# A recommender forward pass on one core: splitting the small tables by identity matmuls instead of VectorE subtractions

## The chip, the core and the metric

The kernel runs on one core of a Trainium2 chip. The metric is the device time of one execution in microseconds (us); lower is better. The kernel before took 5261.35 us, the median of four runs (5259.9 to 5262.66).

The engines named here: TensorE (PE in the profile; PEld is its weight loading), VectorE (DVE), ScalarE (ACT), GpSimd (POOL), which issues the indirect gathers, and SyncE (SP), which issues the plain DMAs. Each works through its own instructions in the order of the program and waits for the others by semaphores. SBUF is the on-chip memory, PSUM the memory that matmuls write.

## The reference

16384 samples. Each takes the mean of 32 rows of a word table (50000 x 300), the means of 20 rows each of three multi-hot tables (1000, 5000 and 10000 rows of 64), and one row each of four one-hot tables (100, 50, 20 and 1000 rows of 64). The 748 features go through a three-layer network. A "wide" scalar per row of the small tables is summed beside it.

```python
tok = word_emb[token_idx].mean(axis=1)
e1 = emb_mh1[mh1_idx].mean(axis=1)        # e2, e3 alike
o1 = emb_oh1[oh1_idx]                     # o2, o3, o4 alike
emb = jnp.concatenate([tok, e1, e2, e3, o1, o2, o3, o4], axis=1)
wide = (wide_mh1[mh1_idx].sum(axis=(1, 2)) + ... + wide_oh4[oh4_idx][:, 0])[:, None]
h = jax.nn.relu(emb @ W1 + b1)            # 748 -> 1024
h = jax.nn.relu(h @ W2 + b2)              # -> 512
h = jax.nn.relu(h @ W3 + b3)              # -> 256
return jax.nn.sigmoid(h @ Wd + bd + wide)
```

## The kernel before

**Tiles and ticks.** The batch is cut into 128 tiles of 128 samples (loop over `t`, line 476). Each tile has 11 steps (`STEPS`, loop over `i`, line 489). This text calls one step a tick and numbers ticks through the tiles: tick 0 is the first step of tile 0, tick 11 the first of tile 1. The order of all instructions is written out by hand (`tc.manual_schedule()`). In one tick the program issues, in this order: the one-hot masks of the next tick (`one_hots`, line 294, VectorE, two instructions), the count matmuls of this tick (`counts`, line 312, twelve matmuls, eight in a tile's last tick) with their eviction by ScalarE (line 319), some steps of the table conversion (only in tiles 0 and 1), the token gathers and sums, a share of the small-table sums of the tile before (`small_sums`, line 337), and, from tile 5 on, a share of the network of the block of four tiles before (`mlp`).

**Tokens.** The 32 word rows of a sample are gathered in 16 groups of two: GpSimd issues two indirect DMAs (line 224), and VectorE adds the two rows to a running sum (lines 211, 213, 215). The adds of a group are issued three groups later (`TOK_LAG`), and there are six buffers `tok_rows`: the first gather of group n+6 needs the buffer of group n, so it waits for the adds of group n. The running sum `own` lies in PSUM, as does the `iota` that the masks are compared with.

**Small tables.** The seven small tables are 138 slices of 128 rows of 65 values (64 and the wide one). A tile's small lookups are turned into counts for every slice row (one-hot masks multiplied on TensorE), and the counts are multiplied with the slices, which lie in SBUF as `terms`: three bf16 terms that together hold twice the f32 value. `small_sums` reads a slice of `terms` for every matmul, from tick 11 on. It takes slices 0 to 15 in tick 11 and reaches slice 134 in tick 19.

**Making the terms.** `convert_tables` fills `terms` while ticks 3 to 17 run, paced by `TABLE_PACE`: `tables_on_chip.to(TABLE_PACE * (t * STEPS + i - 2))` (line 501) advances the generator until it has made that many steps. The tables come in six parts of 23 slices, loaded by SyncE (lines 152 and 158) into two buffers (`raw`, tags "even" and "odd"); VectorE clears the incomplete slices first (line 157). Each part takes three steps: ScalarE casts to bf16 (line 180), then VectorE subtracts the term just made from the f32 rows (line 177) and ScalarE casts the remainder, twice. The next part's load is issued when a part begins, into the buffer of the part before.

**Buffers around it.** The one-hot masks have two buffers, so the masks of tick T+1 wait for the count matmuls of tick T-1. The counts' PSUM tile `pc` has one, so the count matmuls of tick T wait for the eviction of tick T-1. The PSUM tag "ph" has two buffers; the key transposes, the feature transposes and the layers use it, and in ticks 3 to 19 it is free.

Of the kernel before, what the change touches and what calls it, by code (L numbers as in the profile page):

```python
# [8 lines left out]
F32 = mybir.dt.float32  # L9
BF16 = mybir.dt.bfloat16  # L10
# [3 lines left out]
AF = mybir.ActivationFunctionType  # L14
ALU = mybir.AluOpType
AX = mybir.AxisListType

P = 128
N_TOK, TOK_D = 32, 300
N_MH, EMB = 20, 64  # L20
ROW = EMB + 1
# [4 lines left out]
HALF = P // 2  # L26
N_SMALL = 3 * N_MH + 4
ONEHOT = 6
STEPS = -(-HALF // ONEHOT)
CHUNK_WORK = 1  # L30
TABLE_PACE = 1.2
LAYER_TIME = 10


# [12 lines left out]
def kernel(  # L47
# [21 lines left out]
    nc = tc.nc  # L69
# [6 lines left out]
    slices, n_h = {}, 0  # L76
# [6 lines left out]
    const = ctx.enter_context(tc.tile_pool(name="const", bufs=1))  # L83
# [8 lines left out]
    ps_h = ctx.enter_context(tc.tile_pool(name="ps_h", bufs=2, space=bass.MemoryType.PSUM))  # L92
# [17 lines left out]
    ident = const.tile([P, P], F32, name="ident")  # L110
# [3 lines left out]
    scale = const.tile([P, NK], F32, name="scale")  # L114
# [20 lines left out]
    at = 0  # L135
# [4 lines left out]


    terms = const.tile([P, n_h, 3 * ROW], BF16, name="terms")
    PART = n_h // 6

    def load_tables(part0, tag):
        raw = xp.tile([P, PART, ROW], F32, name="raw", tag=tag)
        for f in SMALL:
            table, (h0, h1) = tables[f], slices[f]
            full, rest = divmod(table.shape[0], P)
            a, b = max(h0, part0), min(h0 + full, part0 + PART)  # L150
            if a < b:
                nc.sync.dma_start(
                    out=raw[:, a - part0 : b - part0, :],
                    in_=table[(a - h0) * P : (b - h0) * P, :].rearrange("(h p) d -> p h d", p=P),
                )
            if rest and part0 <= h0 + full < part0 + PART:
                nc.vector.memset(raw[:, h0 + full - part0, :], 0.0)
                nc.sync.dma_start(out=raw[0:rest, h0 + full - part0, :], in_=table[full * P :, :])
        return raw

    def convert_tables():


        tags = ("even", "odd")
        raws = [load_tables(k * PART, tags[k]) for k in range(2)]
        yield
        for part in range(n_h // PART):
            rows = raws[part]
            if 1 <= part < n_h // PART - 1:
                raws.append(load_tables((part + 1) * PART, tags[(part + 1) % 2]))  # L170
            for c in range(3):
                term = [
                    terms[:, part * PART : (part + 1) * PART, k * ROW : (k + 1) * ROW]
                    for k in range(3)
                ]
                if c:
                    nc.vector.scalar_tensor_tensor(
                        rows, rows, 2.0 if c == 1 else 1.0, term[c - 1], op0=ALU.mult, op1=ALU.subtract
                    )
                nc.scalar.activation(term[c], rows, AF.Copy, scale=2.0 if c == 0 else 1.0)  # L180
                yield 1

    w1_sb = const.tile([P, NK, D1], F32, name="w1_sb")
    w2_sb = const.tile([P, M1, D2], F32, name="w2_sb")
# [7 lines left out]
    def load_weights():  # L192
        for k, rows in enumerate(chunk_rows):
            at = 0
            for a, b in rows:
                nc.sync.dma_start(out=w1_sb[at : at + b - a, k, :], in_=w1[a:b, :])
                at += b - a
        nc.sync.dma_start(out=w2_sb, in_=w2.rearrange("(k p) m -> p k m", p=P))
        nc.sync.dma_start(out=w3_sb, in_=w3.rearrange("(k p) m -> p k m", p=P))
        for sb, dram in ((wd_sb, wd), (b1_sb, b1), (b2_sb, b2), (b3_sb, b3), (bd_sb, bd)):  # L200
            nc.sync.dma_start(out=sb, in_=dram)
# [33 lines left out]
    def last_tokens():  # L235
        for group in under_way:
            add_up(*group)
# [19 lines left out]
    def lookup_keys(ix):  # L257

        pairs = NSUB // 2
        low = keyp.tile([P, pairs, 2, N_SMALL], I32, name="low", tag="low")  # L260
        nc.vector.tensor_single_scalar(low, ix, P - 1, op=ALU.bitwise_and)
        nc.vector.tensor_single_scalar(ix, ix, 7, op=ALU.logical_shift_right)
        keys = keyp.tile([P, pairs, 2, 2 * N_SMALL], BF16, name="keys", tag="keys")
        for r in range(pairs):
            view = keys[:, r].rearrange("p w (f c) -> p w f c", f=2)
            nc.vector.tensor_copy(view[:, 0], low[:, r])
            nc.vector.tensor_add(view[:, 1], ix[:, r], first)
        return keys
# [17 lines left out]
    def one_hots(sc, s, i):  # L286

        b = i * ONEHOT
        rows = min(ONEHOT, HALF - b)
        row1 = ohp.tile([P, ONEHOT, P], BF16, name="row1")  # L290
        slice1 = ohp.tile([P, ONEHOT, n_h], BF16, name="slice1")
        for w, (one, n) in enumerate(((row1, P), (slice1, n_h))):
            shape = [P, rows, n // 2, 2]
            nc.vector.tensor_tensor(  # L294
                one[:, 0:rows, :].rearrange("p i (n d) -> p i n d", d=2),
                iota[:, 0:n].rearrange("p (n d) -> p n d", d=2).unsqueeze(1).to_broadcast(shape),
                sc[:, s // 2, w, s % 2, b : b + rows, :].unsqueeze(2).to_broadcast(shape),
                ALU.is_equal,
            )
        return row1, slice1  # L300

    def counts(cnt, hot, i):

        b = i * ONEHOT
        rows = min(ONEHOT, HALF - b)
        n = rows // 2
        pc = ps_c.tile([P, 2, 2, 512], F32, name="pc")
        for k in range(rows):
            for f in range(2):
                half = slice(f * HALF, (f + 1) * HALF)  # L310
                at = k % n * n_h
                nc.tensor.matmul(  # L312
                    pc[:, f, k // n, at : at + n_h],
                    hot[0][half, k, :],
                    hot[1][half, k, :],
                    start=True,
                    stop=True,
                )
        nc.scalar.activation(  # L319
            cnt[:, :, b : b + rows, :].rearrange("l f (g k) h -> l f g (k h)", g=2),  # L320
            pc[:, :, :, 0 : n * n_h],
            AF.Copy,
            scale=0.5,
            saturate=False,
        )
# [116 lines left out]
    def sums_by_step(gen):  # L442
# [5 lines left out]
        n_second = slices["e3"][1] - slices["e2"][0]  # L448
        for i in range(STEPS):

            steps = STEPS - (n_pairs - 1)
            upto = n_first + -(-n_second * i // steps)
# [15 lines left out]
    sizes = [NSUB] * (tiles // NSUB - 1) + [NSUB - 2, 1, 1]  # L468
    it, ix = load_indices(0)
    tables_on_chip = convert_tables()  # L470
    next(tables_on_chip)
    tables_on_chip = Paced(tables_on_chip)
# [3 lines left out]
    for t in range(tiles + 1):  # L476
# [10 lines left out]
        else:  # L487
            last_tokens()
        for i in range(STEPS):
            if t < tiles:  # L490
# [3 lines left out]
                if s == 2 and i == 0 and t + NSUB < tiles + 1:  # L494
                    next_keys = lookup_keys(ix)
                if i < STEPS - 1:
                    hot = one_hots(sc, s, i + 1)
                elif t + 1 < tiles:
                    hot = one_hots(next_sc if s == NSUB - 1 else sc, (s + 1) % NSUB, 0)
                counts(cnt, hot_now, i)  # L500
                tables_on_chip.to(TABLE_PACE * (t * STEPS + i - 2))
                if t == 1 and i == STEPS - 1:
                    load_weights()
# [61 lines left out]
```

## Time and profile before

| | |
|---|---|
| median of four runs | 5261.35 us |
| the profiled execution | 5264.25 us |
| its span, first to last instruction | 5262.4 us |
| PE busy | 5088.7 us, 97% |
| POOL busy | 3887.9 us, 74% |
| DVE busy | 3767.2 us, 72% |
| ACT busy | 2445.6 us, 46% |
| DMA engines | mean 124 GB/s, 0.47 of their time in the middle of the span |
| table casts, ACT L180 | 18 instructions, 128x1495, median 1468 ns, 19.6 to 80.6 us |
| table subtractions, DVE L177 | 12 instructions, 128x1495, median 1707 ns, 21.1 to 78.9 us |
| granted TensorE clock, mean | 0.99 |

How to read it: busy time is the union of an engine's instructions, and the issuing of a gather counts as busy time on POOL although a fixed gap of 0.30 us follows each one. An engine busy for 97% is not necessarily the one that sets the end, since matmul ends are modelled and an engine may keep pace with another. A line such as "idle before, releaser" says which event ended the engine's idle time. The page's seven rows of costliest groups belong to work that goes on in every tile; the table conversion lies in the first 82 us alone.

### The profile page before, as it was taken

The page shows a single profiled execution, that of the slowest core. Times are in us where ns is not written, and L with a number is a line of the kernel's source. Part 1 is how long each engine was busy: PE and PEld are TensorE (multiplying, and loading weights), DVE is VectorE, ACT ScalarE, POOL GpSimd, SP SyncE. Part 2 cuts the span into 40 slices and gives each one's busy share as a digit, 9 for nine tenths or more (in the row PEclk, how much of TensorE's full clock was granted, in tenths as well). Part 3 has the DMA queues.
Part 4 walks back from the last instruction along what each step waited for, and adds up shares of the span by engine and source line. Part 5 has one row for each costly group of instructions (what it writes and reads, how often), then busy time and mean ns, then how long its engine had stood idle before and what let it go on. Part 6 is the DMA issues. An engine that isn't in the chain of part 4 may idle for free.

```text
span 5262.4 us, 104252 instructions
## 1 busy us (share of the span) xinstructions
PE 5088.7 (97%) x41320; PEld 3162.3 (60%) x41320; DVE 3767.2 (72%) x8014; ACT 2445.6 (46%) x1938; POOL 3887.9 (74%) x4103
## 2 busy tenths in 40 slices
PE   4799999999999999999999999999999999999999
PEld 3565565665656656665655666556566556666558
DVE  8777777777777777777777777777777777777752
ACT  5444444444444444444444444444444444444432
POOL 7777777777777777777777777777777777777761
PEclk8899999999999999999999999999999999999999
DMA  6444444444444444444444444444444444444431
GB/s 190 125 125 124 126 126 126 126 125 124 126 126 126 126 124 126 126 126 126 126 124 125 126 126 126 125 124 126 126 126 126 124 126 126 126 126 126 124 99 34
DMA packets 252890, 652.60 MB, mean 124 GB/s; under 512 B 119009, under 2 KB 119524, under 8 KB 252399
## 3 DMA queue, kind: packets, MB, share of 16 engines
q0 software_dynamic: 196608, 629.41, 44.5%
q1 hardware_dynamic: 55791, 16.53, 1.4%
q8 instruction: 323, 5.29, 0.4%
q14 instruction: 168, 1.38, 0.1%
HBM read 645.59 MB, written 0.07 MB: 123 GB/s over the span
## 4 chain that ended last, share of the span: by engine, by line
PE 43%; DMA 21%; DVE 14%; issue 13%; POOL 9%; ACT 0%; DVEq 0%; SPq 0%; POOLq 0%; ACTq 0%
PE ph L388 23%; DMA tok_rows<-in_word_emb_dram,it 21%; PE pg L337 14%; POOL tok_rows L224 9%; PE pc L312 5%; DVE own L215 4%; DVE own L213 2%; DVE slice L294 2%; DVE x L379 1%; DVE row L294 1%; DVE g L343 1%; PE po L413 1%; DVE own L211 0%; DVE g L215 0%; PE po L417 0%
## 5 line engine op out<-in xcount | busy, mean ns | idle before, releaser
L224 POOL DMA_INDIRECT tok_rows<-in_word_emb_dram,it x4096 | 3887.0, 949 | 1294.3 <-issue 735.6
L319 ACT ACTIVATE cnt<-pc 128x1656 fp8e3<-128x1656 f32 (+1 forms) x1408 | 2120.7, 1506 | 2046.7 <-PE pc L312 2037.0
L337 PE MATMUL pg<-terms,cnt 128*128 128x195 bf16 x17664 | 1850.0, 254 | 89.0 <-DVE g L343 86.6
L337 PEld LDWEIGHTS <-cnt 128*128 128x128 fp8e3 x17664 | 1598.6, 144 | 235.8 <-issue 81.9
L388 PE MATMUL ph<-x,w_sb 128*128 128x512 f32 (+5 forms) x3264 | 1467.7, 579 | 3.6 <-DVE x L379 2.8
L215 DVE TENSOR_TENSOR own<-own,tok_rows 128x300 f32<-128x300 f32 x1792 | 857.8, 479 | 679.7 <-DMA tok_rows<-in_word_emb_dram,it 646.0
L388 PE MATMUL ph<-h,w_sb 128*128 128x512 f32 (+2 forms) x2720 | 1211.0, 573 | 0.0
L213 DVE TENSOR_TENSOR own<-own,tok_rows 128x300 f32<-128x300 f32 x1920 | 918.9, 479 | 363.9 <-DMA tok_rows<-in_word_emb_dram,it 311.4
L312 PEld LDWEIGHTS <-row 64*128 64x128 bf16 x16384 | 502.0, 95 | 1038.4 <-DVE slice L294 249.5
L294 DVE TENSOR_TENSOR row<-own,sc 128x768 bf16<-128x768 bf16 (+1 forms) x1408 | 762.3, 541 | 187.9 <-PE pc L312 118.6
L312 PE MATMUL pc<-slice,row 64*128 64x138 bf16 x16384 | 758.8, 224 | 69.0 <-DVE slice L294 35.3
L388 PEld LDWEIGHTS ph<-x,w_sb 128*128 128x128 f32 (+1 forms) x3264 | 563.8, 194 | 410.4 <-issue 398.1
L294 DVE TENSOR_TENSOR slice<-own,sc 128x828 bf16<-128x828 bf16 (+1 forms) x1408 | 797.3, 566 | 0.0
L388 PEld LDWEIGHTS ph<-h,w_sb 128*128 128x128 f32 x2720 | 463.1, 192 | 318.8 <-issue 316.9
L397 ACT ACTIVATE h<-ph,b_sb 128x512 f32<-128x512 f32 (+2 forms) x476 | 315.6, 663 | 687.3 <-PE ph L388 682.3
L343 DVE TENSOR_REDUCE g<-pg 128x130 f32<-128x390 f32 (+1 forms) x512 | 259.0, 506 | 145.2 <-PE pg L337 144.1
L379 DVE TENSOR_SCALAR x<-pt,scale 128x512 f32<-128x512 f32 (+4 forms) x204 | 137.0, 712 | 3.4 <-PE pt L378 2.7
L378 PE MATMUL pt<-ident,g 128*128 128x128 f32 (+1 forms) x768 | 104.4, 275 | 3.0 <-DVE x L379 2.3
L211 DVE TENSOR_TENSOR own<-tok_rows 128x300 f32<-128x300 f32 x128 | 61.7, 482 | 47.6 <-DMA tok_rows<-in_word_emb_dram,it 45.0
L378 PEld LDWEIGHTS pt<-ident,g 128*128 128x128 f32 (+1 forms) x768 | 85.3, 140 | 8.1 <-DVE x L379 6.9
L215 DVE TENSOR_TENSOR g<-own,tok_rows 128x300 f32<-128x300 f32 x128 | 60.2, 470 | 22.8 <-DMA tok_rows<-in_word_emb_dram,it 18.1
L413 PE MATMUL po<-h,wd_sb 128*1 128x512 f32 (+2 forms) x136 | 60.9, 566 | 0.3
(34 smaller groups left out, 290.0 us busy)
## 6 DMA issues: line engine op xcount, KB each, us to landing
tok_rows<-in_word_emb_dram,it POOLq DMA_INDIRECT x4096
ix<-in_idx_dram SPq DMA_DIRECT2D x128, 32.0 KB
w_sb<-in_W_dram SPq DMA_DIRECT2D x6, 512.0 KB
raw<-in_mh_dram SPq DMA_DIRECT2D x3, 747.5 KB
it<-in_idx_dram SPq DMA_DIRECT2D x32, 64.0 KB
w_sb<-in_W_dram SPq DMA_DIRECT2D x1, 2048.0 KB
raw<-in_mh_dram SPq DMA_DIRECT2D x1, 617.5 KB
out_dram<-h SPq DMA_DIRECT2D x31, 2.0 KB
```

The costliest lines, as they stand in the source:

```text
L213: nc.vector.tensor_add(tok_sum, tok_sum, a)
L215: nc.vector.tensor_add(to, tok_sum, b)
L224: nc.gpsimd.indirect_dma_start(out=rows[:, r * TOK_D : (r + 1) * TOK_D], out_offset=None, in_=word, in_offset=bass.IndirectOffsetOnAxis(ap ...
L294: nc.vector.tensor_tensor(one[:, 0:rows, :].rearrange("p i (n d) -> p i n d", d=2), iota[:, 0:n].rearrange("p (n d) -> p n d", d=2).unsque ...
L312: nc.tensor.matmul(pc[:, f, k // n, at : at + n_h], hot[0][half, k, :], hot[1][half, k, :], start=True, stop=True,)
L319: nc.scalar.activation(cnt[:, :, b : b + rows, :].rearrange("l f (g k) h -> l f g (k h)", g=2), pc[:, :, :, 0 : n * n_h], AF.Copy, scale=0 ...
L337: nc.tensor.matmul(pg[:, j, :], by_slice[:, :, h], terms[:, h, :], start=(h == h0), stop=(h == h1 - 1))
L343: nc.vector.tensor_reduce(g[:, at : at + n * ROW].rearrange("p (f d) -> p f d", f=n), pg[:, 0:n, :].rearrange("p f (c d) -> p f d c", c=3) ...
L378: nc.tensor.transpose(pt[:kk, s * P : (s + 1) * P], chunk(g, k), ident)
L379: nc.vector.tensor_scalar(x[:kk, k, 0:n], pt[:kk, 0:n], scale[:kk, k : k + 1], None, ALU.mult)
L388: nc.tensor.matmul(ph[:, 0:n], weights[:kk, k, m * P : (m + 1) * P], src[:kk, k, 0:n], start=(k == 0), stop=(k == len(kks) - 1),)
L397: nc.scalar.activation(dst[:, m, 0:n], ph[:, 0:n], AF.Relu, bias=bias[:, m : m + 1])
```

## The change

The rows of the small tables are no longer changed in place by VectorE. The remainder of a slice is made by TensorE in PSUM: the f32 rows times an f32 identity, plus the finished terms times a bf16 matrix of -0.5 on the diagonal (`minus_half`, made once by VectorE). As the terms hold twice the value, that sum is the value less the terms, and ScalarE casts it from PSUM with a scale of 2. The work goes in pieces of seven slices (455 columns, 20 pieces) in place of parts of 23, three terms of three different pieces in one step: the third term of piece s-2, the second of s-1, the first of s. There are 22 steps. Parts that are loaded together have 21 slices (seven parts, the last of 12), and a part's buffer is loaded anew, for the part after next, when its last piece has its third term. `TABLE_PACE` goes from 1.2 to 1.3, so that the steps lie in ticks 3 to 19: two each in ticks 3, 6, 9, 13 and 16, one in the others.

```diff
 ONEHOT = 6
+SPLIT = 7
+PART = 3 * SPLIT
...
-TABLE_PACE = 1.2
+TABLE_PACE = 1.3
...
     terms = const.tile([P, n_h, 3 * ROW], BF16, name="terms")
-    PART = n_h // 6
+    minus_half = const.tile([P, P], BF16, name="minus_half")
+    nc.vector.tensor_single_scalar(minus_half, ident, -0.5, op=ALU.mult)
...
-        raws = [load_tables(k * PART, tags[k]) for k in range(2)]
+        parts = range(0, n_h, PART)
+        raws = [load_tables(parts[k], tags[k]) for k in range(2)]
         yield
-        for part in range(n_h // PART):
-            rows = raws[part]
-            if 1 <= part < n_h // PART - 1:
-                raws.append(load_tables((part + 1) * PART, tags[(part + 1) % 2]))
-            for c in range(3):
-                term = [
-                    terms[:, part * PART : (part + 1) * PART, k * ROW : (k + 1) * ROW]
-                    for k in range(3)
-                ]
-                if c:
-                    nc.vector.scalar_tensor_tensor(
-                        rows, rows, 2.0 if c == 1 else 1.0, term[c - 1], op0=ALU.mult, op1=ALU.subtract
-                    )
-                nc.scalar.activation(term[c], rows, AF.Copy, scale=2.0 if c == 0 else 1.0)
-                yield 1
+        pieces = []
+        for k, part0 in enumerate(parts):
+            for at in range(part0, min(part0 + PART, n_h), SPLIT):
+                pieces.append((k, at, min(at + SPLIT, part0 + PART, n_h)))
...
+        def make(p, c):
+            if c == 0:
+                nc.scalar.activation(term(p, 0), rows(p), AF.Copy, scale=2.0)
+                return
+            _, a, b = pieces[p]
+            left = ps_h.tile([P, SPLIT, ROW], F32, name="left", tag="ph")[:, 0 : b - a, :]
+            nc.tensor.matmul(left, ident, rows(p), start=True, stop=False)
+            for k in range(c):
+                nc.tensor.matmul(left, minus_half, term(p, k), start=False, stop=(k == c - 1))
+            nc.scalar.activation(term(p, c), left, AF.Copy, scale=2.0)
+
+        for step in range(len(pieces) + 2):
+            for c in (2, 1, 0):
+                if 0 <= step - c < len(pieces):
+                    make(step - c, c)
+            k, _, b = pieces[min(max(step - 2, 0), len(pieces) - 1)]
+            if step >= 2 and b in parts and k + 2 < len(parts):
+                raws.append(load_tables(parts[k + 2], tags[k % 2]))
+            yield 1
```

More of the change, by code (lines that the diff above doesn't have):

```diff
@@ L164, in convert_tables, with term, rows @@
         tags = ("even", "odd")
-        raws = [load_tables(k * PART, tags[k]) for k in range(2)]
+        parts = range(0, n_h, PART)
+        raws = [load_tables(parts[k], tags[k]) for k in range(2)]
         yield
-        for part in range(n_h // PART):
-            rows = raws[part]
-            if 1 <= part < n_h // PART - 1:
-                raws.append(load_tables((part + 1) * PART, tags[(part + 1) % 2]))
-            for c in range(3):
-                term = [
-                    terms[:, part * PART : (part + 1) * PART, k * ROW : (k + 1) * ROW]
-                    for k in range(3)
-                ]
-                if c:
-                    nc.vector.scalar_tensor_tensor(
-                        rows, rows, 2.0 if c == 1 else 1.0, term[c - 1], op0=ALU.mult, op1=ALU.subtract
-                    )
-                nc.scalar.activation(term[c], rows, AF.Copy, scale=2.0 if c == 0 else 1.0)
-                yield 1
+        pieces = []
+        for k, part0 in enumerate(parts):
+            for at in range(part0, min(part0 + PART, n_h), SPLIT):
+                pieces.append((k, at, min(at + SPLIT, part0 + PART, n_h)))
+        def term(p, c):
+            _, a, b = pieces[p]
+            return terms[:, a:b, c * ROW : (c + 1) * ROW]
+        def rows(p):
+            k, a, b = pieces[p]
+            return raws[k][:, a - parts[k] : b - parts[k], :]
+        def make(p, c):
+            if c == 0:
+                nc.scalar.activation(term(p, 0), rows(p), AF.Copy, scale=2.0)
+                return
+            _, a, b = pieces[p]
+            left = ps_h.tile([P, SPLIT, ROW], F32, name="left", tag="ph")[:, 0 : b - a, :]
[11 more added lines that the diff above has]
+            yield 1
     w1_sb = const.tile([P, NK, D1], F32, name="w1_sb")
```

## The prediction

> **What bounds the kernel now.** PE's 97% invites the answer "TensorE". I asked who waits. First the page's group of the gathers, then POOL's waits between 300 and 5000 us:
>
> ```profile
> L224 POOL DMA_INDIRECT tok_rows<-in_word_emb_dram,it x4096 | 3887.0, 949 | 1294.3 <-issue 735.6
> ...
> POOL tok_rows L224 <- issue: 667.7, 2192, 0.3
> POOL tok_rows L224 <- DVE own L215: 292.5, 960, 0.3
> ```
>
> The last number is the longest wait: never above 0.3 us, which is the fixed gap after every gather. So in 4700 us nothing holds POOL up. The gathers' own view from 100 to 5000 us shows the pace:
>
> ```profile
> L224 POOL DMA_INDIRECT tok_rows<-in_word_emb_dram,it x3918: 942/946/1193, 99.2 to 4999.4; - x196
> ```
>
> (4999.4 - 99.2) / 3917 = 1.251 us a gather, 40.0 us a tile of 32. TensorE keeps up with that; it becomes the bound only after about 5018 us, when POOL's gaps grow beyond 0.3, and works off the rest. Hence what POOL loses early moves the end one for one. It does lose early. At 1.251 us the 65th gather would start at 3.20 + 64 x 1.251 = 83.3 us; the timeline has it at 94.22. Of these 10.9 us, 0.15 is the first gather's own length. The rest is seen in the timeline of the first tile (start, duration):
>
> ```profile
> 21.09 1.72 DVE L177 SCALAR_TENSOR_TENSOR raw<-raw,terms 128x1495 f32<-128x1495 f32 x1 [4.21 <-ACT terms L180]
> 22.10 1.52 POOL L224 DMA_INDIRECT tok_rows<-in_word_emb_dram,it  x1 [0.30 <-issue]
> ...
> 24.78 1.71 DVE L177 SCALAR_TENSOR_TENSOR raw<-raw,terms 128x1495 f32<-128x1495 f32 x1
> 25.22 2.08 POOL L224 DMA_INDIRECT tok_rows<-in_word_emb_dram,it  x1 [0.30 <-issue]
> ```
>
> A gather under way when L177 runs ends 0.81 us after L177 does: 21.09 + 1.72 = 22.81, and 22.10 + 1.52 = 23.62; 26.49 and 27.30. It is so for all twelve L177, 0.814 to 0.820 us each time, and no other gather takes over 1.2 us. The excess over 946 ns sums to 10.7 us. Adds and masks (own in PSUM, one SBUF input) leave gathers at 0.95.
>
> **The change, part by part.** *Removed:* twelve L177, 12 x 1.71 = 20.5 us of DVE, and with them the twelve long gathers: -10.7 us on the path, if nothing else delays POOL.
>
> The section "Who interferes with whom" of "SBUF — State Buffer" in the Trainium skill speaks against this: there an elementwise two-input VectorE operation takes only the read side of the port shared with GpSimd, while writing descriptors needs the write side (marked as inferred). By that the gain would be nothing. The twelve ends in this trace decide otherwise for this operation.
>
> *What could delay POOL instead* is the buffer. The first gather of group n+6 waits for the adds of group n. Undelayed, it is due at 3.35 + 2.502 (n+6). Compare today's adds: group 22 (tick 17) ends them at 81.48 us, due 73.4, so with the gap of 0.3 it is 8.4 us late, which today's lost 10.7 covers. Were DVE's schedule unchanged, 8.4 of 10.7 would come back as waits. So the second question is how fast ticks 3 to 19 run now. In tick T the adds follow the masks of T+1, which wait for the counts of T-1: the first adds end about 1.05 (two masks) + 0.98 (two adds) + 0.1 = 2.1 us after those counts. For group 22 the counts of tick 16 must be done by 73.4 - 0.3 - 2.1 = 71.0; before, it was 76.7.
>
> *Added on ACT:* 60 casts of 128x455 for 18 of 128x1495. The trace has no such cast; rows of 128x256 (474 ns) and 128x512 (688) of L397 give 0.64, those of L319 (1091 at 1104, 1548 at 1656) 0.55. Back to back, starts lie 0.1 closer than durations (22.84 + 1.47 against 24.22), so 0.45 to 0.55; I take 0.5, 1.5 a step. A counts' eviction is 1.4 start to start.
>
> *Added on PE,* a step: two f32 matmuls and three bf16 of 455 columns. At full clock L388 starts 512 f32 columns every 429 ns, L337 195 bf16 columns every 87: 0.38 and 0.20, so 1.37 a step. At half clock (granted 0.5, 854 and 164 ns) it is 0.76 and 0.38, 2.67 a step. Counts are 0.54 or 0.87 a tick, 15 matmuls of L337 1.3 or 2.46.
>
> "FP8 and Floating Point Precision" ("TensorE Precision Notes") gives true f32 four passes; 4 x 0.20 would be 0.81, 2.2 a step at full clock, counts 16 about 7 us later than below and some 1 us of waits. L388's 429 ns is 1.9 times the bf16 rate, not 4.
>
> *Which clock?* At 52 to 56 us PE worked 3.5 us of 4; L337 went from 164 to 87 ns there. It fell to half after a stretch at a third of busy time (59.4 to 62.8), rose after 0.85 (72 to 76), and stayed full at 0.65 to 0.8 (96 to 112). In tile 0 at half clock a tick of one step is 0.87 + 2.67 of PE in 3.75 us, 0.95 busy: it should rise. At full clock it is about 0.7 busy and should mostly stay; in tile 1 it is nearly always busy.
>
> *Sum for ticks 3 to 16.* Tick 3's eviction starts at 18.15 as before. Tile 0 has eight ticks and 11 steps, bound by ACT: 7 x 1.4 + 1.0 + 11 x 1.5 = 27.3, and some 1.7 for a cold start; counts 11 done at 47 (before 52.2). Then five ticks with six steps, bound by PE: 5 x (0.54 + 1.3) + 6 x 1.37 + 0.6 for the double step = 18.0; counts 16 at 65. Due 71.0, so 6 us to spare, and no wait. Half clock throughout: 38 us for tile 0 (five ticks of 3.75, three of 6.4, where ACT and PE wait for each other), 5 x 3.33 + 6 x 2.67 = 32.7 for the five ticks, counts 16 at 88.8, 17.8 late. These are the ends; I take the near one, for PE's busy share speaks for the full clock.
>
> *Loads.* A part's load starts when its buffer's last f32 matmul is done and is first read two steps later, 6.5 to 7 us at this pace; a load raises the DMA's rate for about 6 us (28 to 34 us). If late, a cast waits on ACT, behind it the next eviction, the single pc buffer, PE's counts, DVE's masks and adds, and last POOL. Cover: the spare 6 us; gone, four loads at 1 us or less each. VectorE's clears (0.11 us) now wait for that matmul, in ticks 6 and 15, with that tick's adds behind them: adds of tick 15 due 65.6, expected 63.5. SP issues 17 part loads for 16; between them only index loads (tick 11), needed in tick 24, and later weights, needed in tile 5.
>
> *At nothing:* minus_half, one 0.23 us instruction (as L113) in DVE's 3.62 us wait for ix; without that cover 0.23. PE's and ACT's waits in a step cost nothing while counts keep their due times. From tile 2 the program is the same, 10.7 earlier.
>
> Sum: 5264.25 - 10.7 = 5253.55 for the profiled execution. It lies 2.9 above the median of the runs, so 5261.35 - 10.7 = 5250.6.
>
> **Rivals.** (A) the forecast, 5250.6.
> (B) The lock goes, a slot wait takes its place: casts at 0.55, late loads or stretches at half clock put counts 16 some 2 to 10 us after 71.0. For: ACT filled to 3.4 of a tick's 3.64 us, loads just in time. Against: 6 us to spare. At today's schedule 10.7 - 8.4 = 2.3 gained: 5259.0; typically 5254.
> (C) Slower: PE stays at half clock through tile 1, 6.0 us a tick of one step against POOL's 3.64. Counts 18, 14.7 after 88.8, come at 103.5, group 25's adds at 105.6, due 80.6: 25 us late, 14.3 more than today's loss, 5275.6. It decides once these adds pass 80.6 + 10.7 = 91.3. For: half clock in most of 63 to 97 us before. Against: that PE was idle half the time.
> (D) The long gathers do not go with L177, only coincide with it: 5261. Against: twelve of twelve.
>
> **Chances.** A 0.60, B 0.27, C 0.07, D 0.06. A measurement of this kernel tells about 0.2% from no change, 10.5 us here, so A lies on that edge: 0.7 of it counts as faster, 0.42. Within 0.2%: 0.18 of A, B and D, 0.51. Slower: C, 0.07. Range 5249.0 to 5260.0: A with the runs' scatter of 1.4, and B; it leaves out C, D and A's lowest twentieth.
>
> **What will show it.** Right: no gather over 1.2 us before 84 us, the 65th at 83.4, no POOL wait above 0.3 before 5000, counts 11 near 47 and counts 16 near 65, PE's clock full from about 28. B: POOL waits for own L215 above 0.3 in ticks 12 to 19. C: L337 at 164 ns in tile 1. Wrong altogether: gathers stretched under other work, or POOL losing time after tile 2.

## The result, and the profile after

The changed kernel took 5255.95 us (median of 40 runs, 5253.0 to 5258.71), the kernel before beside it 5260.96 (60 runs, 5258.94 to 5265.21): a ratio of 0.999, 95% interval 0.9985 to 0.9994. It is 5.0 us faster, 0.1%, and the interval lies below 1. The forecast was 5250.6, so half of the 10.7 us is missing. The profiled execution took 5255.58 us, its span 5253.8.

In seven of the twelve runs below every kernel, the one before too, took about 7100 to 7180 us, with TensorE pausing again and again (busy 79 to 80% of the span) for a reason that no run shows, so their times say nothing of this change.

First the shape of the whole: the page's group of the gathers, their view from 100 to 5000 us (durations min/median/max), and POOL's waits from 300 to 5000 us (total, times, longest).

```profile
L246 POOL DMA_INDIRECT tok_rows<-in_word_emb_dram,it x4096 | 3875.5, 946 | 1298.4 <-issue 728.9
...
L246 POOL DMA_INDIRECT tok_rows<-in_word_emb_dram,it x3919: 942/946/1246, 99.1 to 4999.6; - x196
...
POOL tok_rows L246 <- issue: 662.9, 2176, 0.3
POOL tok_rows L246 <- DVE own L237: 301.3, 989, 0.3
```

From 100 us on the pace is the old one, (4999.6 - 99.1) / 3918 = 1.251 us a gather, with no wait above 0.3. POOL's busy time fell by 3887.0 - 3875.5 = 11.5 us, so the long gathers are gone. Yet the last gather starts at 5174.4 us in place of 5181.8, and the 65th at 87.02 in place of 94.22, where 83.4 was forecast. What was lost lies before 100 us. The same two views for 18 to 100 us, the kernel before first:

```profile
POOL tok_rows L224 <- DVE own L215: 2.0, 6, 0.4
...
L224 POOL DMA_INDIRECT tok_rows<-in_word_emb_dram,it x58: 940/946/2492, 17.1 to 99.2; - x58
```

```profile
POOL tok_rows L246 <- issue: 12.5, 41, 0.3
POOL tok_rows L246 <- DVE own L237: 6.9, 4, 3.9
...
L246 POOL DMA_INDIRECT tok_rows<-in_word_emb_dram,it x62: 940/946/1059, 17.1 to 99.1; - x62
```

The longest gather is 1059 ns (2492 before), and a wait of up to 3.9 us for the adds has come, where the longest such wait before was 0.4. The timeline shows where it comes from (start, duration, engine, line; in brackets the idle time before and what ended it):

```profile
66.46 0.54 PE L334 MATMUL pc<-slice,row 64*128 64x138 bf16 x12
66.93 1.03 PE L191 MATMUL left<-raw,ident 128*128 128x455 f32 x2
...
67.80 0.56 PE L193 MATMUL left<-terms,minus_half 128*128 128x455 bf16 x2
...
68.05 0.34 DVE L160 MEMSET raw<- 128x65 f32 x4 [4.05 <-PE left L191]
68.20 0.93 PE L191 MATMUL left<-raw,ident 128*128 128x455 f32 x2
68.30 0.45 DVE L235 TENSOR_TENSOR own<-own,tok_rows 128x300 f32<-128x300 f32 x1
68.79 0.48 DVE L237 TENSOR_TENSOR own<-own,tok_rows 128x300 f32<-128x300 f32 x1
68.96 0.36 PE L193 MATMUL left<-terms,minus_half 128*128 128x455 bf16 x1
69.17 1.46 PE L359 MATMUL pg<-terms,cnt 128*128 128x195 bf16 x15
69.54 0.94 POOL L246 DMA_INDIRECT tok_rows<-in_word_emb_dram,it  x1 [3.85 <-DVE own L237]
...
70.56 0.54 PE L334 MATMUL pc<-slice,row 64*128 64x138 bf16 x12
```

Two things are to be seen. In tick 15 VectorE stood 4.05 us at the clear of a raw buffer, waiting for TensorE to have read it, with the adds of group 19 queued behind; these ended at 69.27, and a gather due at 65.99 (0.30 us after the end of the one before) started at 69.54. And each identity matmul over f32 is two instructions (x2): from its start to that of the bf16 matmul after it are 67.80 - 66.93 = 0.87 us, then 68.96 - 68.20 = 0.76. From counts to counts this tick of one step takes 70.56 - 66.46 = 4.10 us, where 0.54 + 1.3 + 1.37 = 3.2 had been forecast and POOL needs 3.64. TensorE is busy for all of 55 to 76 us, at the full granted clock.

Two smaller waits follow, again for the adds: the gather at 90.16 (0.94 us idle, adds of group 27) and this one at 96.65, for group 29:

```profile
95.90 0.48 DVE L237 TENSOR_TENSOR own<-own,tok_rows 128x300 f32<-128x300 f32 x1
...
96.65 0.94 POOL L246 DMA_INDIRECT tok_rows<-in_word_emb_dram,it  x1 [1.78 <-DVE own L237]
```

Over the 0.30 us gap the three cost 3.55, 0.64 and 1.48 us, 5.7 together. Now take each group's lateness as the prediction defined it: the end of its adds, and the gap, against the due time of an undelayed POOL, 3.35 + 2.502 (n+6). Group 19 is 3.7 late, group 27 4.3, group 29 5.8. So 5.7 is not three separate prices but one largest lateness reached in three steps. A gather that is held up once shifts all later ones, and only an even later group costs more.

In the kernel before, group 29's adds ended at 96.28, in the changed one at 96.38, although the counts of tick 16 were done 2.4 us earlier, at 71.1 against 73.5. The ticks behind them were slower: the counts of ticks 17 to 21 were done 0.6 to 1.6 us later than before. From the reduction of the small sums in tick 19 on, VectorE works without a wait up to group 29's adds, through the same instructions in both kernels. The counts of tick 16 and that reduction before, then the reduction in the changed kernel, where VectorE had stood 3.03 us for TensorE's sums:

```profile
72.62 0.87 PE L312 MATMUL pc<-slice,row 64*128 64x138 bf16 x12 [0.72 <-ACT cnt L319]
...
87.80 0.55 DVE L343 TENSOR_REDUCE g<-pg 128x130 f32<-128x390 f32 x1
```

```profile
87.62 0.56 DVE L365 TENSOR_REDUCE g<-pg 128x130 f32<-128x390 f32 x1 [3.03 <-PE pg L359]
```

Before, group 29's lateness, and the largest of 8.4 at group 22, hid under the 10.7 us that the long gathers had cost.

### The profile page after: what moved, and what is told of

It is laid out like the page before. It is cut to its first block, busy times and chain, and to the rows that moved or that the text cites. A ratio compares the mean times of both kernels' runs of the same rounds, so it can differ in the third digit from the quotient of the medians.

```text
span 5253.8 us, 104566 instructions
## 1 busy us (share of the span) xinstructions
PE 5108.5 (97%) x41460; PEld 3171.4 (60%) x41460; DVE 3744.1 (71%) x8003; ACT 2449.6 (47%) x1980; POOL 3876.4 (74%) x4103
## 3 DMA queue, kind: packets, MB, share of 16 engines
q0 software_dynamic: 196608, 629.41, 44.5%
## 4 chain that ended last, share of the span: by engine, by line
PE 32%; DMA 24%; DVE 19%; issue 15%; POOL 9%; ACT 0%; DVEq 0%; SPq 0%; POOLq 0%
DMA tok_rows<-in_word_emb_dram,it 24%; PE ph L410 16%; PE pg L359 10%; POOL tok_rows L246 9%; DVE own L237 5%; PE pc L334 4%; DVE slice L316 3%; DVE own L235 3%; DVE row L316 2%; DVE x L401 2%; DVE g L365 1%; PE po L435 1%; DVE own L233 1%; PE left L191 0%; DVE g L237 0%
## 5 line engine op out<-in xcount | busy, mean ns | idle before, releaser
L246 POOL DMA_INDIRECT tok_rows<-in_word_emb_dram,it x4096 | 3875.5, 946 | 1298.4 <-issue 728.9
L410 PE MATMUL ph<-x,w_sb 128*128 128x512 f32 (+5 forms) x3264 | 1452.3, 573 | 2.4 <-DVE x L401 0.7
```

The source lines that it names most:

```text
L246: nc.gpsimd.indirect_dma_start(out=rows[:, r * TOK_D : (r + 1) * TOK_D], out_offset=None, in_=word, in_offset=bass.IndirectOffsetOnAxis(ap ...
L410: nc.tensor.matmul(ph[:, 0:n], weights[:kk, k, m * P : (m + 1) * P], src[:kk, k, 0:n], start=(k == 0), stop=(k == len(kks) - 1),)
```

## The experiments

Two questions: is it the two SBUF operands that hold a gather up, and is it TensorE's f32 price, or the place of the adds, that gave half back? For the runs near 5260 us, "lost" is what the first 100 gathers took beyond 1.2505 us each (the first gather's 0.15 in it).

| kernel | largest lateness, us (group) | lost, us | 65th gather, us | median, us |
|---|---|---|---|---|
| before | 8.4 (22) | 10.95 | 94.2 | 5261.0 |
| changed | 5.8 (29) | 5.90 | 87.0 | 5255.95 |
| plain subtraction | 8.4 (22) | 10.96 | 94.1 | 5260.9 |
| operand from PSUM | 9.6 (22) | 10.31 | 93.0 | 5261.4 |
| adds first | 5.6 (29) | 5.72 | 86.2 | 5256.65 |
| bf16 identity | none late | 0.17 | 83.4 | 5251.3 |
| third term on VectorE, adds first | none late | 0.09 | 83.3 | 5249.3 |

### Another operation with two SBUF operands

The kernel before, every second subtraction written plainly:

```diff
-                if c:
+                if c == 1:
                     nc.vector.scalar_tensor_tensor(
-                        rows, rows, 2.0 if c == 1 else 1.0, term[c - 1], op0=ALU.mult, op1=ALU.subtract
+                        rows, rows, 2.0, term[0], op0=ALU.mult, op1=ALU.subtract
                     )
+                elif c == 2:
+                    nc.vector.tensor_tensor(rows, rows, term[1], op=ALU.subtract)
```

> The kernel before with its second subtraction of each part (the one with scale 1.0) written as a plain VectorE tensor_tensor of the same two SBUF operands, 128x1495 f32; the first subtraction stays a scalar_tensor_tensor and is the control. Theory 1, two SBUF operands hold the gather's issue up whatever the operation: the gathers under all twelve subtractions end 0.8 us after them, six under each kind, excess 10 us in all; if the first tiles set the time as in the runs so far, it stays that of the kernel before (5261). Theory 2, only scalar_tensor_tensor does it (the Trainium skill, SBUF - State Buffer, Who interferes with whom, has two-input elementwise operations leave descriptor writing alone, marked there as inferred): six long gathers of up to 2.5 us stay, under the first subtractions, and those under the tensor_tensor take 0.94 to 0.95 us; lost to the lock then some 5 us, and with adds up to 8.4 us late the gain is 10.95 - 8.4 = 2.5 us at most, 5258.5.

It took 5260.89 us, ratio 1.0 (0.9988 to 1.0011). The first two subtractions and the gathers under them, in its timeline:

```profile
21.01 1.72 DVE L177 SCALAR_TENSOR_TENSOR raw<-raw,terms 128x1495 f32<-128x1495 f32 x1 [4.21 <-ACT terms L182]
22.01 1.53 POOL L226 DMA_INDIRECT tok_rows<-in_word_emb_dram,it  x1 [0.30 <-issue]
...
24.70 1.71 DVE L181 TENSOR_TENSOR raw<-raw,terms 128x1495 f32<-128x1495 f32 x1
25.14 2.08 POOL L226 DMA_INDIRECT tok_rows<-in_word_emb_dram,it  x1 [0.30 <-issue]
```

22.01 + 1.53 is 0.81 us after 21.01 + 1.72, and 25.14 + 2.08 is 0.81 after 24.70 + 1.71. It is so for all twelve, 0.814 to 0.820 us. Theory 1 holds; theory 2, the reading of the Trainium skill's "SBUF — State Buffer" ("Who interferes with whom"), falls for both operations.

The traces show two things more. In all twelve cases the gather that was held began while the operation ran; the eleven that were already under way when one began took 0.940 to 0.948 us in the kernel before. And neither a long operation nor a second input is needed. The longest gather of the changed kernel before 100 us began under a tile's first add, which reads both rows from SBUF, and ended 0.81 us after it too:

```profile
55.64 0.48 DVE L233 TENSOR_TENSOR own<-tok_rows 128x300 f32<-128x300 f32 x1
55.87 1.06 POOL L246 DMA_INDIRECT tok_rows<-in_word_emb_dram,it  x1 [0.30 <-DVE slice L316]
```

Count in the whole of the kernel before the gathers that began at least 0.05 us into an operation, and early enough that a hold of 0.81 us beyond its end would show. All 18 under such first adds ended 0.81 us after them, and all 8 under the int32 mask and shift of lines 261 and 262, which read a single operand, from SBUF, 0.81 to 0.82 after those. Of 1703 under operations that read an operand from PSUM, none took over 0.96 us.

### The same operation with one operand in PSUM

```diff
                     nc.vector.scalar_tensor_tensor(
-                        rows, rows, 2.0 if c == 1 else 1.0, term[c - 1], op0=ALU.mult, op1=ALU.subtract
+                        rows,
+                        rows,
+                        2.0 if c == 1 else 1.0,
+                        own[:, 0:ROW].unsqueeze(1).to_broadcast([P, PART, ROW]),
+                        op0=ALU.mult,
+                        op1=ALU.subtract,
                     )
```

> The kernel before, its twelve subtractions reading their second operand from PSUM (the running sum, repeated over the slices) in place of the term in SBUF; the real subtraction is left out, operation, shape and order stay. Lock theory: operations of 1.71 us as before, gathers under them 0.94 to 0.95 us. Then by the largest-lateness theory the adds' lateness of up to 8.4 us (group 22), which the 10.8 us of the lock covered, comes out as waits for own and the gain is 10.95 - 8.4 to 8.6, some 2.3 us: 5258.7. Rival (the lost 10.7 us come back whole): 5250.3. Rival (any VectorE work of this length holds gathers): 5261.

5261.4 us, ratio 1.0001 (0.9992 to 1.001): no gain, the figure of the third theory, but not for its reason.

```profile
24.89 1.70 DVE L177 SCALAR_TENSOR_TENSOR raw<-raw,own 128x1495 f32<-128x1495 f32 x1
25.33 0.95 POOL L229 DMA_INDIRECT tok_rows<-in_word_emb_dram,it  x1 [0.30 <-issue]
26.62 1.47 ACT L185 ACTIVATE terms<-raw 128x1495 bf16<-128x1495 f32 x1 [0.90 <-DVE raw L177]
27.89 0.94 POOL L229 DMA_INDIRECT tok_rows<-in_word_emb_dram,it  x1 [1.61 <-DVE own L220]
```

The operation still takes 1.70 us, and the gather under it 0.95; none of the gathers under the twelve operations takes over 950 ns. So in this operation neither VectorE's being busy nor its writing to SBUF holds a gather; it is the second operand's lying in SBUF. (The edit also turns that operand from bf16 to f32, repeated over the slices. The third-term kernel below reads a bf16 operand from SBUF beside one from PSUM, and holds no gather either.) The next gather then waits 1.61 us for the adds: the lock's loss has come back as waits. POOL lost 10.3 us, against a largest lateness of 9.6 at group 22. That lateness had been expected at 8.4 to 8.6; the size missed, as far as the timeline tells, because the edit made VectorE itself slower. The next adds write what this operation reads, and begin after it, 22.82 against its end at 22.79, where before they began 0.08 ahead of it, 22.73 against 22.81. That is 0.11 us for each of twelve operations, 1.3 in all. (Its profiled execution lost another 14 us after 100 us, which the median does not show; only its first 100 us are read here.)

This is the clearest sight of why half the forecast's gain could vanish: taking the lock away alone is worth next to nothing while the adds are that late.

### The adds ahead of the table steps

```diff
                 counts(cnt, hot_now, i)
+                toks.to(n_groups * (i + 1) / STEPS)
                 tables_on_chip.to(TABLE_PACE * (t * STEPS + i - 2))
                 if t == 1 and i == STEPS - 1:
                     load_weights()
-                toks.to(n_groups * (i + 1) / STEPS)
```

> The changed kernel with the tick's token gathers and adds issued ahead of its table steps, so that no add of a tick is queued behind the clear of a raw buffer. Theory (what GpSimd loses is the largest lateness of any group's adds, so the three waits seen, 3.55, 0.64 and 1.48 us, are steps up to one largest lateness of 5.8 us at group 29): the wait at 69.5 us goes, the loss comes back at groups 27 to 30, and the time stays at that of the changed kernel, 5255 to 5256.5. Rival (the waits add up, each with its own cause): 3.55 us less, 5252.4.

5256.65 us, ratio 0.9991 (0.9982 to 1.0) to the kernel before. POOL's waits from 18 to 100 us:

```profile
POOL tok_rows L246 <- issue: 13.1, 43, 0.3
POOL tok_rows L246 <- DVE own L237: 5.6, 4, 1.9
POOL tok_rows L246 <- DMA tok_rows<-in_word_emb_dram,it: 1.6, 1, 1.6
```

The wait of 3.85 us is gone: the adds of group 19 end at 64.85 in place of 69.27. Waits of 1.25, 1.59, 1.33 and 1.48 us over the gap, at 79.6, 83.7, 90.0 and 96.5 us, sum to 5.65. (The 1.6 put down to a DMA is such a wait: the gather started at 79.58, and the adds of its buffer had ended at 79.31.) Group 29's adds end at 96.20, 5.6 late, as in the changed kernel. The order of the waits changed, their sum and the time did not, as the theory of the largest lateness has it. What looked like the largest wait was worth nothing by itself.

### The f32 price taken out

```diff
-            nc.tensor.matmul(left, ident, rows(p), start=True, stop=False)
+            nc.tensor.matmul(left, ident_bf, term(p, 0), start=True, stop=False)
```

> The changed kernel with the f32 identity matmul replaced by one bf16 matmul of a finished term (the f32 rows are left out of the remainder). Theory (the f32 matmul, two instructions and 0.8 us for 455 columns in place of the forecast's 0.38, put the adds of groups 19 to 32 late): a step is 1.3 us of TensorE shorter, counts of tick 16 done by 65, no add late by over 0.5 us, and the time is 5250 to 5251.5. Rival (ScalarE's casts or the late clears set the ticks): 5254 to 5256.

5251.26 us, ratio 0.9982 (0.9973 to 0.9991). The groups of line 191 and TensorE's busy time from 18 to 86 us, first in the changed kernel, then here, with POOL's longest wait for adds and its gathers from 18 to 100 us (the second kind of row: length, then PE, PEld, DVE, ACT and POOL busy, granted clock, DMA share, GB/s):

```profile
L191 PE MATMUL left<-raw,ident 128*128 128x455 f32 x76 | 39.6, 604 | 0.4 <-ACT terms L194 0.4
...
18.00:86.00 68.00, 67.30 (x453) 37.38 (x450) 39.70 (x85) 52.84 (x76) 48.61 (x53) 1.00 0.79 211
```

```profile
L191 PE MATMUL left<-terms,ident_bf 128*128 128x455 bf16 x38 | 14.4, 378 | 7.8 <-ACT terms L194 4.7 <-ACT terms L187 2.1
...
18.00:86.00 68.00, 51.31 (x494) 32.49 (x491) 48.33 (x110) 57.34 (x81) 51.25 (x56) 0.95 0.91 255
...
POOL tok_rows L246 <- DVE own L237: 0.6, 2, 0.3
...
L246 POOL DMA_INDIRECT tok_rows<-in_word_emb_dram,it x67: 942/946/949, 17.1 to 99.6; - x67
```

38 products are 76 instructions in f32 and 38 in bf16, and TensorE falls from 67.3 to 51.3 busy of 68 us while it does as much or more of everything else. Counts of tick 16 are evicted from 61.2 us on in place of 71.1, no group's adds are late, POOL has no wait above 0.3 us, and the 65th gather starts at 83.38, where the forecast had put it. The casts on ScalarE and the clears on VectorE are all still there, so they did not set the ticks. The edit also frees the raw buffers earlier, as no matmul reads the f32 rows now; but in the changed kernel no cast of these rows had waited for a load (0.0 us idle before the 19 casts of line 187), and the run with the adds first had shown the place of the clears worth nothing. So the f32 price is the cause.

### The third term on VectorE

The second remainder is left in PSUM for a step, and VectorE makes the third term from it (one operand in PSUM) in place of two matmuls of TensorE and a cast of ScalarE. The adds come first, as above.

```diff
+            if c == 2:
+                nc.vector.scalar_tensor_tensor(
+                    term(p, 2), lefts[p], 2.0, term(p, 1), op0=ALU.mult, op1=ALU.subtract
+                )
+                return
...
+            lefts[p] = left
             nc.tensor.matmul(left, ident, rows(p), start=True, stop=False)
-            for k in range(c):
-                nc.tensor.matmul(left, minus_half, term(p, k), start=False, stop=(k == c - 1))
-            nc.scalar.activation(term(p, c), left, AF.Copy, scale=2.0)
+            nc.tensor.matmul(left, minus_half, term(p, 0), start=False, stop=True)
+            nc.scalar.activation(term(p, 1), left, AF.Copy, scale=2.0)
```

> The changed kernel with the third term made by VectorE straight from the second's remainder in PSUM (one operand in PSUM, so no lock by theory) and the adds issued ahead of the table steps: one f32 and one bf16 matmul a step in place of two and three, one cast less on ScalarE, one VectorE operation of 455 columns (some 0.6 us) more. Theory: the step is 1.2 us of TensorE shorter, no gather over 1.1 us, no add late, 5250 to 5251.5, below both kernels. Rival (the added VectorE work or the lock makes adds late again): 5254 or more.

5249.31 us, ratio 0.9979 (0.997 to 0.9988): 11.7 us below the kernel before, and the lowest median of all. POOL's waits and gathers from 18 to 100 us, and the new operation's group from 18 to 86:

```profile
POOL tok_rows L251 <- DVE own L240: 1.8, 6, 0.3
POOL tok_rows L251 <- DVE own L242: 1.8, 6, 0.3
...
L251 POOL DMA_INDIRECT tok_rows<-in_word_emb_dram,it x67: 942/946/961, 17.1 to 99.6; - x67
...
L191 DVE SCALAR_TENSOR_TENSOR terms<-left,terms 128x455 bf16<-128x455 f32 x19 | 11.7, 626 | 2.9 <-ACT terms L199 2.8
```

20 VectorE operations with one operand in SBUF lengthen no gather, and of the first 44 groups none has its adds less than 3.3 us early.

Whether this needs the adds ahead was to be told by the same kernel without that move:

> The changed kernel with the third term made by VectorE from the second's remainder in PSUM, the order of the adds left as the change has it; it tells which of the two edits of the version with adds first brought 5249.3. Theory (the f32 and bf16 matmuls taken away do it; no add is late then, so their place in the tick is worth nothing): no wait for own above 0.3 us before 5000 us, 5249 to 5251. Rival (the adds have to be ahead of the clears and of the new VectorE operation): the adds of group 19 or of the groups after 27 come late again, 5252 or more.

It took 7162.59 us beside 7148.25 of the kernel before, 1.0022 (1.0008 to 1.0037), and so does not tell. Its longest gather from 18 to 100 us, 950 ns, says once more that this operation holds none up; the question of the order stays open.

### The earlier runs of the same kernels

Four of the kernels above had been tried before, in six runs that took 7120 to 7145 us and decide nothing on the time. The adds first, twice, 1.0018 (1.0001 to 1.0034) and 1.0006 (0.9991 to 1.0022):

> The changed kernel, with the token gathers and adds of a tick issued ahead of its table steps, so that no add stands behind a clear of a raw buffer. In the changed kernel POOL waits three times before 100 us: 3.55 us for the adds of group 19 (behind the clear in tick 15), 0.64 and 1.48 us for those of groups 27 and 29. Theory 'largest lateness': POOL's loss is not the sum of single waits but the largest lateness of any adds against POOL's undisturbed due times, and that is 5.8 us at group 29, which no clear precedes; then the first wait shrinks to under 1 us, the later ones grow to some 5 us together, and the time stays at 5255.9 (within 1). Rival 'the clear costs its wait': the 3.55 us come off, 5252.4.

> The changed kernel with the token gathers and adds of a tick issued ahead of its table steps (the kernel of e1_adds_first again, whose run went at 7134 us beside 7121 of the kernel before: in that call every kernel lost some 4 us of TensorE time every 14 us or so through the whole span, and nothing of the first 100 us can be read from it). Theory 'largest lateness': POOL's loss is the largest lateness of any adds against POOL's undisturbed due times, 5.8 us at group 29, which no clear precedes; so the first wait (3.55 us, group 19) shrinks to under 1 us, the later ones grow to some 5 us together, and the time stays at 5255.9 (within 1). Rival 'the clear costs its wait': the 3.55 us come off, 5252.4.

The bf16 identity, 1.0002 (0.9986 to 1.0018). Between two pauses of TensorE its ticks of one step take 2.78 us (evictions at 69.32 and 72.1), where the changed kernel's take 4.1:

> The changed kernel, with the f32 matmul of every remainder (two instructions of 0.43 us) replaced by one bf16 matmul of the same columns (identity in bf16 times the first term); it leaves the f32 rows out, so the second and third terms are wrong. It takes the suspected cost, TensorE's f32 passes, and nothing else away: per step 2 x (0.82 - 0.2) = 1.2 us less of PE. Theory 'PE is what makes ticks 11 to 19 late': a tick of one step falls from 4.1 us to about 3, counts 16 come near 65 instead of 70.6, all adds keep their due times, POOL waits under 0.5 us in all, 5250.6 (5250 to 5252). Rival 'the ticks are set by ScalarE's 60 casts or the loads': ticks stay near 4, 5255 to 5256.

The third term on VectorE with the adds first, twice, 1.0005 (0.999 to 1.0019) and 1.0009 (0.9988 to 1.0029):

> The changed kernel with the third term made by VectorE from the remainder in PSUM (twice the remainder less the second term, written straight to bf16: one SBUF operand, no lock), in place of a second f32 matmul group and a ScalarE cast, and with the adds of a tick ahead of its table steps. Per step PE loses an f32 matmul and two bf16 ones (1.25 us), ACT a cast (0.5), DVE gains about 0.55. Theory 'PE makes the ticks late': a tick of one step falls below POOL's 3.64 us, POOL waits under 0.5 us before 100 us, 5250.6 (5250 to 5252), with the computation complete. Rival 'VectorE's new instruction waits for ScalarE and holds the adds': POOL waits of some us remain, 5253 to 5257.

> The kernel of e5_third_on_vector_adds_first again (third term by VectorE from the remainder in PSUM, adds of a tick ahead of its table steps), because TensorE was held up all through that call. Theory 'PE makes the ticks late': a tick of one step falls below POOL's 3.64 us, POOL waits under 0.5 us before 100 us, 5250.6 (5250 to 5252). Rival 'VectorE's new instruction waits for ScalarE and holds the adds': POOL waits of some us remain, 5253 to 5257.

The operand from PSUM, 1.0026 (1.0009 to 1.0043). Its twelve operations took 1702 to 1714 ns and the gathers that overlap them 940 to 948 ns, much as in the later run:

> The kernel before, with the second operand of its VectorE subtraction read from PSUM (65 columns of the iota tile, broadcast) in place of the term in SBUF: same operation, shape and engine, but one SBUF operand in place of two; it leaves the real subtraction out, so the terms are not those of the tables. Theory: the lock between this operation and the gathers goes (no gather over 1.2 us before 84 us), but VectorE's schedule is about as before, whose largest lateness was 8.4 us at group 22, so POOL still waits about 8.4 us in place of 10.7: 5261.0 - 2.3 = 5258.7. Rival 'the lock is the whole loss': -10.7, 5250.3. Rival 'the operation blocks the gathers whatever its operands': gathers as long as before, 5261.0.

## Why the prediction was half right

**What bounds the kernel, and one for one.** Right. POOL's loss in its first 100 gathers accounts for the times to within 1.0 us: 5261.0 less what a kernel lost below 10.95 gives 5255.95, 5255.8, 5250.2 and 5250.1 for the changed kernel, adds first, bf16 and third on VectorE, and 5255.95, 5256.65, 5251.26 and 5249.31 were measured.

**The lock.** Right, and now shown: another operation with two SBUF operands does it too, the same one with an operand in PSUM does not. All twelve long gathers went, and rival D falls.

**What could delay POOL instead.** The due times, and the warning that 8.4 us of lateness lay hidden, were right; they were to be read as a largest lateness, which the operand from PSUM and the adds first both show. The 76.7 us that it gives for tick 16 of the kernel before was misread: there tick 17's counts end, and tick 16's were done at 73.5. So the lead that it forecast there was 8.5 us, and not 11.7.

**Added on PE: the term that failed.** "0.38" for an f32 matmul of 455 columns. It measured 0.76 to 0.87, at the full clock. The 429 ns of L388 were the mean spacing of *instructions*, and an f32 matmul of the program is two. The page had the sign of it: x3264 for 34 blocks of 48 matmuls, 1632. So "1.9 times the bf16 rate, not 4" dismissed a rule that was right. The Trainium skill's "FP8 and Floating Point Precision" ("TensorE Precision Notes") gives true f32 four passes, and this trace agrees, with 0.76 to 0.87 us against 4 x 0.20. The sum that the prediction made by that rule, counts 16 about 7 us later and some 1 us of waits, had the counts right (65 forecast, 71 measured, 72 by the rule), but not the waits, which were 5.7. It stopped at tick 16. From counts to counts, ticks 16, 17 and 18 took 6.25, 4.09 and 3.82 us against POOL's 3.64 a tick, and the lateness grew from 1.5 us at group 22 to 5.8 at group 29.

**Clock.** Right: full from 25.8 us to 90.7 (28 forecast). Rival C falls. In tile 0 TensorE was busier than the 0.7 forecast, 19.6 of the 20 us from 26 to 46; whether the clock would have stayed full at 0.7 is not shown.

**Added on ACT.** 0.55 to 0.58 us a cast, 0.5 forecast; with the same 60 casts in the bf16 run no add was late, so this cost nothing. Counts 11 were evicted from 48.8 us on (47 forecast; 44.5 with the bf16 identity), so that slip goes with the f32 price as well.

**Loads and clears.** The clear of tick 15 was named with its adds behind it, due 65.6, expected 63.5; they came at 69.27. The queue was right, the time wrong by the f32 price, and adds first showed that the clear's place cost nothing beside the later groups. The part loads kept no gather waiting.

**The rival that came.** B: lock gone, a slot wait in its place. Its price, typically 5254, at most 5259.0, held 5255.95, but it had named slow casts, late loads or half clock as the way there. The casts did take 0.55 us and cost nothing, and the other two did not come. So the time lies in the stated range by B's share of it, and that it does is no proof of the working: the forecast itself, 5250.6, was 5.35 us too low, for want of the f32 price.

## What to carry to other kernels

Divide a group's instruction count by the program's own loop before taking a duration as the price of one operation. Where an engine paced by its own work is held up by buffers, compute each buffer's lateness against the undelayed pace: the loss is the largest of them. Removing a smaller one gains nothing, and removing a stall that covered them gains only the difference. And where GpSimd issues gathers that set the time, let long VectorE operations that read SBUF alone read one operand from PSUM, but see first what the gathers will wait for next.

## What the hardware showed that was not expected

A plain VectorE subtraction of two SBUF operands held a gather's issue until 0.814 to 0.820 us after its end, exactly like the form with a scalar; reading one operand from PSUM at the same duration (1.70 us) left gathers at 943 to 950 ns. Only gathers that began while the operation ran were held, and a one-operand int32 operation on SBUF held them in the same way. An f32 matmul appears in the trace as two instructions, 0.76 to 0.87 us together for 455 columns, where one of bf16 starts 0.20 before the next.
